# Lending result rooms to the Winograd weights, later residual copies, and ScalarE alone at the last eviction

## The chip, the cores and the metric

The kernel runs on one core of a Trainium2 chip. The metric is the time of one execution on the device in microseconds; several runs are made and their median is taken. One more execution is profiled, and everything called a view (busy shares, waits, the chain of waits, timelines, DMA queues) comes from that one. PE is TensorE, PEld its weight loads, DVE is VectorE, ACT is ScalarE, POOL is GpSimd, SP is SyncE, which only issues DMAs.

## The reference

Input is x, 16 images of 1024 channels by 32x32 pixels, all in float32. Two bottleneck layers follow each other:

```python
# layer 0
h = relu(bn(conv1x1(x, w_conv1)))            # 1024 -> 256
q, k = relu(bn(conv1x1(h, wq))), relu(bn(conv1x1(h, wk)))
v = bn(conv1x1(h, wv))
attn = softmax over the 9 neighbours of q . (k_neighbour + position), 32 heads of 8
h = relu(bn(sum over neighbours of attn * v_neighbour))
x = relu(bn(conv1x1(h, w_conv3)) + x)        # 256 -> 1024
# layer 1
y = relu(bn(conv1x1(x, w1)))                 # 1024 -> 256
y = relu(bn(conv3x3(y, w2)))                 # 256 -> 256
out = relu(bn(conv1x1(y, w3)) + x)           # 256 -> 1024
```

## The kernel before

The work is a written list of stages, run one after the other. A letter and an image name a stage: `C8` is the first convolution of image 8 (kind `conv1`, 8 parts, one for each 128 input channels, matmul line 389), `Q8` its q and k projections (kind `qk`, 5 parts, line 475), `V8` its v projection (kind `v`, 2 parts), `F3` layer 0's last convolution of image 3 fused with layer 1's first (kind `fused`, lines 421 and 389), `W0` the 3x3 convolution of images 0 to 3 in Winograd form (kind `wino`, 18 steps, line 822), `U0` layer 1's last convolution of image 0 (kind `u3`, 8 parts, line 421). `S12` to `S15` (kind `pairs`, lines 1263 and 1251) do that for the last four images with fewer products; their last piece is `Quad.finish`. The list begins `P0 P1 P2 P3 C4 F0 Q4 V4 F1 P5 P6 F2 P7 F3 C8 Q8 W0 V8 C9 U0 Q9 V9 U1 U2 U3`; P stands for C, Q and V of one image.

Attention and the Winograd transforms run on VectorE beside these stages. What is done after each part is written out by hand as a string of letters (`ORDER`), which `side.passes()` reads, one word after each part.

*Weights.* A queue holds the weight pieces in the order of use. `more_weights` takes the first, takes a room of 128x1024 and issues its load on SP (line 132). Rooms come from `wpool` with 5 buffers, or, for pieces named `U` (the transformed 3x3 weights, 18 pieces of 512 KB in a Winograd stage), from the list `spare` if it holds something. `done_with`, called after the last product that uses a piece, gives a lent room back to `spare` and calls `more_weights`. Before the changed version only `lend_rooms` fills `spare`, ahead of W12, with two other tiles cut in four.

*Results.* `rpool` has 4 buffers (`RESULTS`) for the outputs of the fused, `u3` and `pairs` stages. From C8 to the end of C9 no stage of that kind runs.

*Data.* `more_loads` issues loads on GpSimd (line 361) into the 5 rooms of `xpool` in the order of use, as rooms come free: `x` for C, `s` and `r` (residuals) for F and U, `V` (transformed images) for W. A transform on VectorE (lines 751 to 762) stores its `v` pieces through SP (line 787), and a V load waits for those stores.

*Residuals.* PSUM is used as 4 tiles of 128x1024 (`ps`), handed out in turn. Before the products of F or U, ScalarE copies the residual into a PSUM tile (`Expand.seed`, line 412) and the matmuls add to it. The first two such copies of a stage are issued in the last two parts of the stage before, each ahead of its part. Then `result` (line 440) evicts on ScalarE, with bias and ReLU, and GpSimd stores (line 441).

*Projection.* If an image is over 4 and its `Q` stage is followed by `V` and then C or U (`together`), its parts are: k, k, q, q, first v; then the `V` stage: part 0 the products of q with the position table (`positions`, line 521) and their copy (line 529), part 1 the second v. Each projection takes a PSUM tile and is evicted on ScalarE (line 488).

*Tail.* `Quad.finish` splits the last result in two halves in two PSUM tiles; before the change ScalarE evicts the first (line 1334) and VectorE the second (line 1337), and the second is stored by two DMAs of 64 partitions, on ACT and SP.

Of the kernel before, what the change touches and what calls it, by code (L numbers as in the profile page):

```python
# [8 lines left out]
F32 = mybir.dt.float32  # L9
AF = mybir.ActivationFunctionType  # L10
ALU = mybir.AluOpType
AX = mybir.AxisListType

P = 128
B, C, H, W = 16, 1024, 32, 32
HW = H * W
# [8 lines left out]
RELU = AF.Relu  # L25
CHUNKS, RESULTS = 5, 4
# [46 lines left out]
def sa_bottleneck_kernel(ctx: ExitStack, tc: tile.TileContext, x, w1t, wqkvt, w3t, u1t, u2t, u3t, params, out):  # L73
    nc = tc.nc
# [6 lines left out]
    rpool = ctx.enter_context(tc.tile_pool(name="rpool", bufs=RESULTS))  # L81
# [16 lines left out]
    queue, pieces, last_use = [], {}, {}  # L98

    def source(name, half):  # L100

        if name[0] == "U":
            return uw[int(name[1]), half]
        if name in ("w3", "u3"):
            return ws[name == "u3", half]
        if name[1] == "1":
            src = {"w1": w1t, "u1": u1t}[name].rearrange("(c p) n -> p c n", p=P)
            return src[:, half * NC // 2 : (half + 1) * NC // 2]
        at = {"wqk": slice(0, 2 * WID), "wv": slice(2 * WID, 3 * WID)}[name]
        return wqkvt.rearrange("(c p) n -> p c n", p=P)[:, :, at]  # L110

    def more_weights():

        if not queue:
            return
        key = name, of, half = queue.pop(0)
        if spare and name[0] == "U":
            t = lent[key] = spare.pop(0)
        else:
            t = wpool.tile([P, HW], F32, tag="w", name=f"{name}{half}_{of[0]}")  # L120
        src = source(name, half)
        n, k = src.shape[-1], 1
        for d in src.shape[1:-1]:
            k *= d
        view = t[:, : k * n].rearrange("p (c n) -> p c n", n=n)
        if len(src.shape) == 4:
            view = t.rearrange("p (m j o) -> p m j o", m=NW, j=2)
        if of[1] == 0 and name == "w1":
            for part in (slice(0, 1), slice(1, k)) if half == 0 else (slice(0, k),):
                nc.sync.dma_start(view[:, part], src[:, part])  # L130
        else:
            nc.sync.dma_start(view, src)
        pieces[key] = view
# [10 lines left out]
    spare, lent, late_room = [], {}, {}  # L144

    def lend_rooms():

        late_room["qc"] = apool.tile([P, HEAD_DIM, JPIX], F32, tag="qc", name="qc").rearrange("p d w -> p (d w)")
        for t in (late_room["qc"], kp.rearrange("p n r w -> p (n r w)")):
            spare.extend([t[:, :HW], t[:, HW : 2 * HW]])  # L150
        for _ in range(len(spare)):
            if queue and queue[0][0][0] == "U":
                more_weights()

    now = [0]

# [166 lines left out]
    def halves(half):  # L323
        return slice(half * HALF, (half + 1) * HALF)
# [613 lines left out]
    class Side:  # L938
# [71 lines left out]
        def finish(self, b):  # L1010
            self.passes()
            while any(job[0] == b for job in self.jobs):
                self.attention()
# [11 lines left out]
    for text in (  # L1025
# [5 lines left out]
        for word in text.split():  # L1031
            b, _, of = word[1:].partition(":")
            for letter in "CQV" if word[0] == "P" else word[0]:
                kind = {"C": "conv1", "Q": "qk", "V": "v", "F": "fused", "W": "wino", "U": "u3", "S": "pairs"}[letter]
# [6 lines left out]
    def together(b):  # L1041
        at = [(kind, c) for kind, c, of in stages].index(("qk", b))
        return b > FIRST and [kind for kind, c, of in stages[at + 1 : at + 3]] in (
            ["v", "conv1"], ["v", "u3"]
        )
# [185 lines left out]
    class Quad:  # L1231
# [65 lines left out]
        def finish(self, before, last_one):  # L1297
            self.product(1)
            self.add(0, 0, 1)
            before.product(2)  # L1300
            last_one.close()
            before.product(3)
            before.result(0, before.ends)
            self.product(6)
            self.add(1, 0, 6)
            self.room((7, 4))
            self.product(7)
            self.add(1, 1, 7)
            last_one.product(2)
            self.product(5)  # L1310
            self.split = []
            for n in range(2):
                self.add(n, 1, 5)
                t = psum.tile([P, HW], F32, tag="ps", name="ps")
                t = t.rearrange("p (b x) -> p b x", b=2)[:, :, : HALF // 2].rearrange("p b (j n) -> p b j n", j=2)
                self.split.append(t)
                seed = self.r[0].rearrange("p (b j n) -> p b j n", b=2, j=2)[:, :, :, n * HALF // 4 :][:, :, :, : HALF // 4]
                if n:
                    nc.vector.tensor_copy(t, seed)
                else:  # L1320
                    nc.scalar.activation(t, seed, AF.Identity)
            self.product(4)
            self.add(1, 0, 4)
            self.result(1, self.r[1])
            last_one.product(3)
            last_one.result(0, last_one.ends)
            t = rpool.tile([P, HW], F32, tag="r", name="result")
            for n in range(2):
                self.product(2, n)
                self.product(3, n)  # L1330
                to = t[:, halves(n)].rearrange("p (n b j) -> p n b j", b=2, j=2)
                of = self.split[n].rearrange("p b j n -> p n b j")
                if n == 0:
                    nc.scalar.activation(to, of, RELU, bias=self.shift[0], scale=1.0)
                    nc.sync.dma_start(self.to[0][:, halves(0)], t[:, halves(0)])
                else:
                    nc.vector.tensor_scalar(to, of, self.shift[0], 0.0, ALU.add, ALU.max)
            nc.scalar.dma_start(self.to[0][: P // 2, halves(1)], t[: P // 2, halves(1)])
            nc.sync.dma_start(self.to[0][P // 2 :, halves(1)], t[P // 2 :, halves(1)])

    def late_sums():

# [53 lines left out]
    hooks = {}  # L1396

    def run(at):
        now[0] = at
        kind, b, of = stages[at]  # L1400
        then = seeds(at + 1)
        for after in stages[at : at + 3]:
            if after[0] == "fused":
                next_fused[0] = after[1]
                break
        fetch_attended()
        if kind == "u3" and not late_room and any(s[0] == "wino" and s[1] == B - NK for s in stages[at + 1 : at + 3]):
            lend_rooms()
        if kind == "fused":
            parts, count = fused(b, of, then), 2 * NC  # L1410
        elif kind == "pairs":
            parts, count = late, len(of)
        elif kind == "u3":
            parts, count = last_sum(b, of, then), len(of)
        elif kind == "conv1":
            parts, count = first_conv(b), NC
        elif kind == "qk":
            parts, count = projections.setdefault(b, project(b)), 5
        elif kind == "v":
            parts, count = projections[b], 2  # L1420
        else:
            side.finish_firsts()
            if b == B - NK:
                late_weights()
            parts, count = winograd_conv(b), 18
        alone = kind not in ("fused", "u3", "pairs")
        for part in range(count):
            if alone and then and part >= count - 2 and kind != "wino":
                into, which = then[part - count + 2]

                if which not in into.ahead:
                    into.seed(which)
            next(parts)
            if part == 0 and kind == "fused" and stages[at + 1][0] == "fused":
                next_fused[0] = stages[at + 1][1]
            fetch_attended()
            side.passes()
            if (kind, b, part) in hooks:
                hooks[kind, b, part]()
        if kind == "wino":  # L1440
            made.extend((b + k, n) for k in range(NK) for n in range(NW))
            for into, which in then:
                into.seed(which)
# [11 lines left out]
    def at_first():  # L1455
        warm_up()
        more_weights()
        more_loads()
        nc.scalar.dma_start(par, params)
        more_weights()  # L1460
        norms()
        load_taps(0)
        more_weights()
        load_taps(1)
        more_weights()
        member_table()
        nc.gpsimd.memset(kp, 0.0)
        load_scaled()
        scale_rows()
        position_table()  # L1470
        side.first(winograd_weights())
        side.first(scale_weights())
        hooks["conv1", 2, 0] = clear_hidden

    at_first()
    for at in range(len(stages)):
        run(at)
# [40 lines left out]
```

## Time and profile before

| | us |
|---|---|
| median of 3 runs | 2364.34 |
| lowest, highest | 2363.7, 2369.66 |
| profiled execution, whole | 2365.22 |
| profiled execution, span of the core | 2363.5 |
| PE busy in the span | 2349.9 |
| DVE busy | 2155.0 |
| ACT busy | 916.1 |
| POOL busy | 491.2 |

The span runs from the first to the last instruction of the program; 1.7 us of the profiled execution lie outside it. The ends of matmuls are modelled, so two matmuls in a row overlap slightly in the timeline, and starts are better to compare than ends. A row of the waits gives who waited, for what, the total, how often and the longest. In a timeline the columns are start, duration, engine, line, operation, names, shapes and count, and in brackets the idle time before with what ended it. In the chain of waits they are start, duration and what the program's end depended on then. The trace's granted PE clock was 0.999 throughout.

### The profile page before, as it was taken

How to read it: one execution, taken by the hardware profiler on the slowest of the kernel's cores; microseconds unless marked ns; L12 is line 12 of the kernel's file. 1: busy time of each engine (PE TensorE's matmuls, PEld its weight loads, DVE VectorE, ACT ScalarE, POOL GpSimd, SP SyncE). 2: the span in 40 equal slices, each digit the busy share in tenths (PEclk: the TensorE clock that was granted, in tenths of full speed). 3: DMA queues.
4: the chain of work that ended last, by engine and by line, in shares of the span. 5: the costliest groups of instructions: out<-in, count | busy, mean ns of one | idle time of the engine just before them, and what ended most of it. 6: DMA issues, size and time to landing. Idle time of an engine off the chain costs nothing.

```text
span 2363.5 us, 18841 instructions
## 1 busy us (share of the span) xinstructions
PE 2349.9 (99%) x6252; PEld 1140.5 (48%) x6252; DVE 2155.0 (91%) x1771; ACT 916.1 (39%) x872; POOL 491.2 (21%) x901
## 2 busy tenths in 40 slices
PE   9999999999999999999999999999999999999998
PEld 4444444444475444444466444444467444444843
DVE  4899999999989999999989999999989999967686
ACT  3323342324122574443122574324222463444266
POOL 2212121212121331111121232111111231111222
PEclk9999999999999999999999999999999999999999
DMA  9968687878797998687887998688787897699887
GB/s 365 375 211 301 245 289 250 286 271 273 262 350 250 343 389 301 218 266 242 256 313 270 330 387 317 225 273 288 262 294 273 328 376 245 211 327 329 316 310 289
DMA packets 295584, 691.63 MB, mean 293 GB/s; under 512 B 20800, under 2 KB 165184, under 8 KB 286784
## 3 DMA queue, kind: packets, MB, share of 16 engines
q0 software_dynamic: 120032, 471.66, 54.7%
q1 hardware_dynamic: 174800, 217.54, 28.3%
q10 hardware_dynamic: 656, 1.23, 0.2%
q8 instruction: 50, 0.82, 0.1%
q14 instruction: 46, 0.38, 0.0%
HBM read 415.32 MB, written 275.03 MB: 292 GB/s over the span
## 4 chain that ended last, share of the span: by engine, by line
PE 95%; DMA 2%; DVE 2%; ACT 0%; issue 0%; DVEq 0%; SPq 0%; ACTq 0%
PE ps L389 36%; PE ps L421 33%; PE ps L475 13%; PE ps L822 9%; PE ps L1263 4%; DMA U<-uw 1%; DMA uw<-u 1%; DMA g<-in_u2t_dram 1%; PE ps L521 0%; DVE z L848 0%; DVE y L848 0%; ACT kp L488 0%; DVE prod L620 0%; DMA x<-in_x_dram 0%; DVE u L287 0%
## 5 line engine op out<-in xcount | busy, mean ns | idle before, releaser
L389 PE MATMUL ps<-result,u 128*128 128x512 f32 x1024 | 457.9, 592 | 0.0
L421 PE MATMUL ps<-a,w 128*128 128x512 f32 x1024 | 457.7, 592 | 0.0
L389 PE MATMUL ps<-x,w 128*128 128x512 f32 x1024 | 443.3, 593 | 0.7 <-DMA x<-in_x_dram 0.6
L677 DVE TENSOR_TENSOR acc<-e,bnv 128x2048 f32<-128x2048 f32 x144 | 327.5, 2283 | 18.4 <-ACT e L659 15.4
L421 PE MATMUL ps<-y,u 128*128 128x512 f32 x768 | 331.1, 592 | 0.0
L620 DVE TENSOR_TENSOR prod<-qc,bnk 128x2048 f32<-128x2048 f32 x144 | 324.0, 2287 | 1.8
L440 ACT ACTIVATE result<-ps,par 128x1024 f32<-128x1024 f32 x128 | 142.4, 1113 | 457.3 <-PE ps L421 394.4
L389 PEld LDWEIGHTS ps<-x,w 128*128 128x128 f32 x1024 | 194.6, 190 | 246.6 <-issue 243.6
L421 PEld LDWEIGHTS ps<-a,w 128*128 128x128 f32 x1024 | 194.6, 190 | 244.9 <-issue 243.5
L389 PEld LDWEIGHTS ps<-result,u 128*128 128x128 f32 x1024 | 194.3, 190 | 245.4 <-issue 238.0
L695 DVE TENSOR_TENSOR acc<-acc 128x2048 f32<-128x2048 f32 x128 | 293.4, 2292 | 4.4
L421 PEld LDWEIGHTS ps<-y,u 128*128 128x128 f32 x768 | 145.9, 190 | 183.3 <-issue 181.1
L475 PE MATMUL ps<-h,wqk 128*128 128x512 f32 x512 | 222.4, 592 | 0.5 <-ACT h L1095 0.5
L441 POOL DMA_DIRECT2D r<-result x128 | 68.7, 537 | 596.9 <-ACT result L440 592.9
L625 DVE TENSOR_TENSOR prod<-prod 128x2048 f32<-128x2048 f32 (+1 forms) x80 | 166.2, 2077 | 2.2
L475 PEld LDWEIGHTS ps<-h,wqk 128*128 128x128 f32 x512 | 97.1, 190 | 123.4 <-issue 111.2
L440 ACT ACTIVATE result<-ps,bn_sh 128x1024 f32<-128x1024 f32 x96 | 106.7, 1112 | 105.3 <-PE ps L421 103.9
L1095 ACT ACTIVATE h<-ps,par 128x1024 f32<-128x1024 f32 x32 | 38.4, 1202 | 260.8 <-PE ps L389 260.8
L412 ACT ACTIVATE ps<-s 128x1024 f32<-128x1024 f32 x128 | 131.3, 1025 | 15.1 <-DMA s<-in_x_dram 12.6
L488 ACT ACTIVATE kp<-ps,par 128x1024 f32<-128x1024 f32 x64 | 77.3, 1209 | 147.7 <-PE ps L475 118.5
L361 POOL DMA_DIRECT2D x<-in_x_dram x126 | 67.0, 533 | 275.5 <-PE ps L389 206.3
L845 ACT ACTIVATE z<-ps 128x1024 f32<-128x1024 f32 x48 | 49.1, 1024 | 179.3 <-PE ps L822 133.3
(373 smaller groups left out, 2655.3 us busy)
## 6 DMA issues: line engine op xcount, KB each, us to landing
s<-in_x_dram POOLq DMA_DIRECT2D x128, 512.0 KB, 5.9
r<-result POOLq DMA_DIRECT2D x128, 512.0 KB, 4.6
x<-in_x_dram POOLq DMA_DIRECT2D x126, 512.0 KB, 5.3
out_dram<-result POOLq DMA_DIRECT2D x126, 512.0 KB, 6.8
r<-r POOLq DMA_DIRECT2D x111, 512.0 KB, 7.0
v<-v SPq DMA_DIRECT2D x96, 408.0 KB, 4.8
U<-uw SPq DMA_DIRECT2D x60, 512.0 KB, 5.6
bnk<-kp SPq DMA_DIRECT2D x32, 680.0 KB, 6.9
```

The source lines that it names most:

```text
L389: nc.tensor.matmul(ps[n][:, halves(half)], wt[:, c % (NC // 2), n * P : (n + 1) * P], src[:, halves(half)], start=(c == first), stop=(c == ...
L412: nc.scalar.activation(ps, loaded.pop((self.kind, self.b, o)), AF.Identity)
L421: nc.tensor.matmul(self.ahead[o][:, halves(half)], pieces[key][:, n, o % (NC // 2) * P :][:, :P], self.src[:, n, halves(half)], start=Fals ...
L440: nc.scalar.activation(to_, ps, RELU, bias=self.shift(o), scale=1.0)
L475: nc.tensor.matmul(ps[:, halves(half)], pieces[key][:, m, at : at + P], h[:, m, halves(half)], start=(m == 0), stop=(m == NW - 1),)
L488: nc.scalar.activation(dst, src, func, bias=col(f"L0_conv_{name}_b", n), scale=col(f"L0_conv_{name}_s", n),)
L620: nc.vector.tensor_tensor(by_row(t[:, two]), by_row(qc), kc[:, :, i : i + JROWS, j : j + W], ALU.mult)
L625: nc.vector.tensor_add(u[:, :, 0:4], u[:, :, 0:4], u[:, :, 4:8])
L677: nc.vector.tensor_tensor(by_row(dst), rows(e[:, k, :]).unsqueeze(1).to_broadcast([P, HEAD_DIM, JROWS, W]), vc[:, :, i : i + JROWS, j : j ...
L695: nc.vector.tensor_add(acc, acc, t)
L822: nc.tensor.matmul(acc[i][:, at, :, n, :], pieces[key][:, m, at, n * P : (n + 1) * P], v[:, at, :, m * (TILES + TR) :][:, :, :TILES], star ...
L1263: nc.tensor.matmul(ps, w, by, start=i in (1, 7), stop=True, skip_group_check=True)
```

## The change

There are three edits.

1. After part 2 of stage C8 a hook, `lend_results`, runs four times over: it moves the first `U` piece of the queue to the front, takes a tile of `rpool`, puts it into `spare` and calls `more_weights`. During W0 `done_with` hands these four rooms on to further `U` pieces. At the end of every Winograd stage `spare` is emptied.
2. For a `V` stage that is `together` and followed by a `u3` stage (V9, V12, V15), the two first residual copies are issued later: the first after part 0 (the position products), the second after part 1.
3. In `Quad.finish` ScalarE evicts both halves; the first is stored by SP as before, the second by ACT in one DMA of 128 partitions.

```diff
+    def lend_results():
+
+        for _ in range(RESULTS):
+            at = [key[0][0] for key in queue].index("U")
+            queue.insert(0, queue.pop(at))
+            spare.append(rpool.tile([P, HW], F32, tag="r", name="lent"))
+            more_weights()
...
                 of = self.split[n].rearrange("p b j n -> p n b j")
-                if n == 0:
-                    nc.scalar.activation(to, of, RELU, bias=self.shift[0], scale=1.0)
-                    nc.sync.dma_start(self.to[0][:, halves(0)], t[:, halves(0)])
-                else:
-                    nc.vector.tensor_scalar(to, of, self.shift[0], 0.0, ALU.add, ALU.max)
-            nc.scalar.dma_start(self.to[0][: P // 2, halves(1)], t[: P // 2, halves(1)])
-            nc.sync.dma_start(self.to[0][P // 2 :, halves(1)], t[P // 2 :, halves(1)])
+                nc.scalar.activation(to, of, RELU, bias=self.shift[0], scale=1.0)
+                by = nc.scalar if n else nc.sync
+                by.dma_start(self.to[0][:, halves(n)], t[:, halves(n)])
...
-            if alone and then and part >= count - 2 and kind != "wino":
-                into, which = then[part - count + 2]
+            late_seeds = kind == "v" and together(b)
+            if alone and then and part >= count - (1 if late_seeds else 2) and kind != "wino":
+                into, which = then[0 if late_seeds else part - count + 2]
 
                 if which not in into.ahead:
                     into.seed(which)
             next(parts)
+            if late_seeds and then and part == count - 1:
+                into, which = then[1]
+                into.seed(which)
...
         if kind == "wino":
+            spare.clear()
             made.extend((b + k, n) for k in range(NK) for n in range(NW))
...
         hooks["conv1", 2, 0] = clear_hidden
+        for b, part in ((8, 2),):
+            hooks["conv1", b, part] = lend_results
```

## The prediction

> **What bounds the kernel now.** I read the page's busy shares first: TensorE is busy 99% of the span, so all that any edit can return is the idle time of PE, 2363.5 - 2349.9 = 13.6 us, start and tail included.
>
> ```profile
> PE 2349.9 (99%) x6252; PEld 1140.5 (48%) x6252; DVE 2155.0 (91%) x1771; ACT 916.1 (39%) x872; POOL 491.2 (21%) x901
> ```
>
> The waits of PE name where it stands still in mid-span; two of these rows are what the diff touches.
>
> ```profile
> PE ps L822 <- DMA U<-uw: 1.5, 1, 1.5
> PE ps L822 <- issue: 1.3, 1, 1.3
> ...
> PE ps L475 <- ACT kp L488: 1.0, 3, 0.3
> ...
> PE ps L822 <- ACT z L845: 0.2, 1, 0.2
> ```
>
> Third, the PE timeline of the first Winograd stage (W0, line 822). A step of 16 matmuls normally starts 3.45 us after the one before:
>
> ```profile
> 675.46 3.62 PE L822 MATMUL ps<-V__1_2446,U 128*128 128x256 f32 x16
> 680.61 3.69 PE L822 MATMUL ps<-V__2_2461,U 128*128 128x256 f32 x16 [1.54 <-DMA U<-uw]
> 684.14 3.62 PE L822 MATMUL ps<-V__2_2534,U 128*128 128x256 f32 x16
> ```
>
> 680.61 - 675.46 = 5.15, so 1.70 us is lost here, and 0.08 more in the step after. The chain of waits says why the fifth weight is late:
>
> ```profile
> 665.73 0.02 SPq L132
> 665.74 0.03 issue
> 665.77 14.70 DMA U<-uw
> ```
>
> Its load is issued only when the key weights' room comes free and takes 14.70 us in a full queue (DMA share over 1.0 from 658 to 690 in the windows). The stage lasts 664.99 to 729.55 = 64.56 us; W4, without a stall, 1207.29 to 1269.56 = 62.27. The excess is 2.29: the 1.78 above, and 0.52 around the step at 725.99, where ScalarE's copy waits for VectorE (line 848).
>
> Fourth, a projection followed by a `u3` stage (V9, V12, V15), on PE and then on ACT:
>
> ```profile
> 808.61 1.09 PE L521 MATMUL ps<-q,pos 64*32 64x512 f32 x16
> 810.03 3.70 PE L475 MATMUL ps<-h,wv 128*128 128x512 f32 x8 [0.33 <-ACT kp L488]
> 813.57 16.90 PE L421 MATMUL ps<-y,u 128*128 128x512 f32 x39
> ```
>
> ```profile
> 808.76 1.21 ACT L488 ACTIVATE kp<-ps,par 128x1024 f32<-128x1024 f32 x1 [2.28 <-PE ps L475]
> ```
>
> From the position products to the next stage: 813.57 - 808.61 = 4.96 us. P10, which has no residual copies there, takes 1164.98 - 1160.42 = 4.56. So each of three such places loses 0.40.
>
> Last, the tail:
>
> ```profile
> 2355.71 1.21 DVE L1291 TENSOR_SCALAR result<-bnk,bn_sh 128x1024 f32<-128x1024 f32 x1
> ...
> 2355.88 0.69 ACT L1334 ACTIVATE result<-ps,bn_sh 128x512 f32<-128x512 f32 x1
> ...
> 2356.85 0.73 DVE L1337 TENSOR_SCALAR result<-ps,bn_sh 128x512 f32<-128x512 f32 x1
> ...
> 2357.62 0.55 ACTq L1338 DMA_DIRECT2D out_dram<-result  x1
> 2357.86 1.18 SPq L1339 DMA_DIRECT2D out_dram<-result  x1
> ```
>
> PE ends at 2356.43, but VectorE is still on the 1024-wide eviction and starts the last half at 2356.85; SP issues the last store at 2357.86, which needs 4.6 us (DMA view): 2362.5.
>
> **What the Trainium skill says.** "DMA: Bandwidth & Descriptors", section "Anatomy of one DMA — SWDGE (gpsimd) path": a semaphore wait of a DMA is held on the issuing sequencer; the engines only drain queues. The trace agrees: SP stood 17.6 us on `a<-acc` (line 699) until 634.03, and the second `U` load behind it left at 634.46. Same page, "Issuing engines are not separate DMA queues": SP's and GpSimd's transfers interleave on the same 16 engines. The trace agrees: in the W0 crowd U loads took 14.7 and V loads up to 11.3 us, against medians of 7.6 and about 6 for the stretch.
>
> **The change part by part.**
>
> *Lent rooms.* After part 2 of image 8's first convolution four U loads of 512 KB come on SP, behind `a<-acc`, so at about 634.5 to 636.5; their four rooms (last stored at 617.47, that store landing some 3 us later) are free. The order of SP's queue in the changed kernel puts them there, then one U, then the six `v<-v` stores. So 5 of W0's weights land by about 645 and the fifth no longer waits for room: the step at 680.61 may start at 675.46 + 3.45 = 678.91. What is late next? (a) ScalarE's copies: that of the third step ends at 677.76 + 1.02 = 678.78, just in time; that of the fourth, held by VectorE, ends at 681.46 + 1.02 = 682.48, while its bank is wanted at 682.36: up to 0.2 lost. (b) V data of the sixth step: issued 670.72, 10.4 us to landing = 681.1, wanted at 682.4, 1.2 to spare. (c) Later steps have 2 us and more. Also, U loads in W0 now wait for the same step that frees a lent room, one fewer is in flight around 668.7, so (b) should rather come earlier. VectorE's last chain starts at 699.26 after 2.70 idle, released through ScalarE by PE; it moves with PE, so the 0.52 stays. Gain 1.78 - 0.2, taken as **1.5** (bounds 0 and 2.1). Added DMA bytes: none; 2.1 MB move to 634-650.
>
> What they are moved past: six `v<-v` stores (643.18 to 653.28) and the two `bnk` stores. Unused DMA share from 638 to 650 is 0.25, 0.52 and 0.57 of 4 us each = 5.4 us; four loads at the 403 GB/s or so of a full queue need 2.1/0.403 = 5.2 us. They just fit. VectorE waits once (1.08 us at 646.20) for such a store; I allow 1 us of delay. Image 8's x loads, the last issued at 633.44 and wanted at 646.7, have 5 us over.
>
> *Residual copies.* Three places. With the position products' bank taken before the first copy, the last v product gets the bank of the second q product, evicted by 1345.29 + 1.20 or its like, over 3 us earlier, and not that of v's first part. Removes 0.33 of wait and the slower restart: 3 x 0.40 = **1.2** (bounds 0.9 and 1.3). The second copy now follows v's last eviction: v's last product ends near 813.2, eviction 1.21 to 814.5, copy 1.02 to 815.5, wanted by the second product at 813.2 + 3.43 = 816.6; 1.1 to spare. Behind it on ScalarE stand a third copy (816.5, wanted at 820.0) and the first result (its products end at 816.6). On GpSimd one residual load passes behind five position stores (2.85 us): later by about 3 us, wanted over 10 us later. Nothing on PE.
>
> *Tail.* VectorE loses its 0.73; ScalarE evicts the second half right after the first, at about 2356.50, done 0.69 later at 2357.2 and not 2357.58. One store of 256 KB goes from ScalarE at 2357.2; SP loses its third. With the 4.2 to 4.6 us that stores of 128 and 256 KB took there, landing is 2361.4 to 2361.8 against 2362.5. The bytes are the same and the engines were full until 2361, so I take **0.7** (0.3 to 1.1).
>
> Sum: 1.5 + 1.2 + 0.7 = 3.4 us. The profiled execution had 2365.22 (span 2363.5 and 1.7 around it), so 2361.8 on its scale; it stood 0.9 over the median of the runs, 2364.34, on whose scale I predict 2360.9. Does a gain at 680 survive to the end? VectorE idles 13.5 us at 2075-2089 and 4.2 at 2152, and attention outputs arrive 20 us and more before their stages, so later stages move with PE.
>
> **The rivals.**
>
> *The stall moves on.* In W12, which already borrows rooms for its weights, PE stood 1.3 us ("issue" above) in the same sixth step, for a V load. If in W0 that V load, or the copy held by VectorE, ends last by as much, the lent rooms give nothing: 1.9 us from the rest, 2362.4. For it: the spare time is 1.2 us only. Against: W0's GpSimd queue has no output stores, W12's had several.
>
> *The loads crowd out the stores.* If the whole 5.2 us lands ahead of the `v<-v` stores, the transform on VectorE waits, the sixth V load lands at 686.3 for 682.4, and 3.9 is lost where 1.78 was: +2.1 in W0, +0.2 in all, slower from 5.0 us of delay on, and up to 2366.4 should the tail and the copies also return nothing. For it: only 0.2 us of unused share is left over. Against: most of the burst drains before 643.18.
>
> *The tail doesn't move*, because 1.5 MB of stores are in flight from 2356 on whoever evicts: 2361.6; part of the forecast's range.
>
> **How the numbers follow.** Forecast 0.62 (2359.5 to 2362.0), moved stall 0.20, crowd-out or some wait of its kind 0.18. The range 2358.8 to 2366.0 takes in the bounds and the crowd-out. About 0.3% (7.1 us) is what a measurement of this kernel can tell from no change. PE's idle time in the touched places is under 6 us, so faster by that much has 0.03; slower by that much needs crowding beyond the price above, which I give 0.09; within, 0.88.
>
> **What would show it.** Right: no `DMA U<-uw` row among PE's waits, W0 at 62.8 us or so, 4.56 us at each of the three projections, the last store landing under 6 us after PE's end. Wrong: a wait of line 822 for V or z over 1 us, V loads of W0 issued later than 663.41, a new wait of line 421 for a residual copy.

## The result, and the profile after

The changed kernel takes **2371.52 us** (median of 7 runs, 2370.04 to 2376.23) against 2364.34 before: 7.2 us slower, ratio 1.0035 with a 95% interval of 1.0025 to 1.0045. The forecast was 2360.9, 3.4 us faster. The profiled execution has a span of 2368.5 us, 5.0 more than before.

Busy shares, from the page after:

```profile
PE 2351.1 (99%) x6252; PEld 1142.1 (48%) x6252; DVE 2155.1 (91%) x1770; ACT 916.7 (39%) x873; POOL 491.2 (21%) x901
```

No engine has more work to speak of; PE is idle 17.4 us and not 13.6. The waits of PE after (who waited, for what, total, times, longest) name the place:

```profile
PE ps L830 <- ACT z L853: 6.3, 2, 6.0
PE ps L483 <- ACT h L1103: 1.6, 1, 1.6
PE ps L1462 <- DVE warm L1459: 1.3, 1, 1.3
PE ps L830 <- issue: 1.1, 1, 1.1
```

The edits move the lines by 8: L822 is L830 now, L845 (the z copy) L853, L475 L483. The U wait and the three waits of L475 for `kp` have gone, as forecast. But a wait of 6.0 us for a z copy (ScalarE copies a product out of PSUM, and PE may write there again) stands in W0, where 0.2 stood. The timeline of PE in W0, after:

```profile
675.93 3.62 PE L830 MATMUL ps<-V__1_2454,lent 128*128 128x256 f32 x16
685.57 5.46 PE L830 MATMUL ps<-V__2_2469,lent 128*128 128x256 f32 x16 [6.02 <-ACT z L853]
690.87 3.62 PE L830 MATMUL ps<-V__2_2542,U 128*128 128x256 f32 x16
```

The weights of the fifth step are `lent` and on time. Its V load is on time too: it landed at 677.03. Its place in PSUM is not. The step starts 9.64 us after the one before (5.15 in the kernel before), and then takes 5.30 to the next start, not 3.45. W0 lasts 665.47 to 736.29 = **70.82 us** against 64.56. The chain of waits, after, leads back from there:

```profile
667.15 0.53 POOL V__2_2469 L369
667.68 1.52 POOL q L556 x2
669.20 0.70 POOL pos L541
669.90 1.60 POOL pos L547 x3
671.50 12.77 DMA pos<-by_offset
...
684.49 1.03 ACT z L853
```

`V_1_2` is the V load of the fifth step (here V__2_2469, in the kernel before V__2_2461), `V_2` that of the sixth. Read upward: the z copy waits for a position store of image 8 to land, since that store still reads the room (`zpool`, three rooms) that z takes; the store stands on GpSimd's queue behind the q stores and `V_1_2`, which left at 667.15. In the kernel before, by GpSimd's timeline:

```profile
663.41 0.53 POOL L361 DMA_DIRECT2D V__2_2461<-v  x1 [9.17 <-DMA v<-v]
```

Ahead of `V_1_2` the chain after names a U load that left at 657.48. That is not what released it, since the U load landed at 667.68, when `V_1_2` had left. The sixth v store, which `V_1_2` waits for, left at 657.03 and landed at 666.51 (653.28 and 662.86 before). So two of the prediction's signs of being wrong are there, a z wait over 1 us and a V load later than 663.41. Why that store was late is on VectorE, in its timelines before and after:

```profile
646.20 1.01 DVE L762 TENSOR_TENSOR v<-form 128x816 f32<-128x816 f32 x1 [1.08 <-DMA v<-v]
```

```profile
649.95 1.01 DVE L770 TENSOR_TENSOR v<-form 128x816 f32<-128x816 f32 x1 [4.93 <-DMA v<-v]
```

The transform waits 4.93 us and not 1.08 for its first store to land (the v pieces lie in `zpool` too). That store left SP at 643.08 (643.18 before) and landed at 649.85 (646.1 before). Last, the windows before and after, four microseconds each (length; busy time of PE, PEld, DVE, ACT and POOL; PE clock, DMA share, GB/s):

```profile
634.00:638.00 4.00, 4.00 (x10) 1.74 (x10) 3.90 (x7) 0.00 (x0) 0.00 (x0) 1.00 0.91 256
638.00:642.00 4.00, 4.00 (x11) 1.72 (x10) 3.93 (x5) 0.00 (x0) 0.00 (x0) 1.00 0.75 309
642.00:646.00 4.00, 4.00 (x11) 1.85 (x10) 3.04 (x4) 0.00 (x0) 0.00 (x0) 1.00 0.48 141
646.00:650.00 4.00, 4.00 (x11) 1.68 (x10) 3.74 (x4) 1.21 (x1) 0.00 (x0) 1.00 0.43 128
```

```profile
634.00:638.00 4.00, 4.00 (x11) 1.79 (x10) 3.90 (x6) 0.00 (x0) 0.45 (x1) 1.00 1.00 323
638.00:642.00 4.00, 4.00 (x10) 1.71 (x9) 3.93 (x5) 0.00 (x0) 0.00 (x0) 1.00 1.01 373
642.00:646.00 4.00, 4.00 (x11) 1.80 (x10) 2.94 (x4) 0.00 (x0) 0.00 (x0) 1.00 1.01 406
646.00:650.00 4.00, 4.00 (x11) 1.81 (x10) 0.05 (x1) 0.89 (x1) 0.00 (x0) 1.00 0.92 241
```

The DMA engines are full until 646, where before they had a share of 0.91, 0.75 and 0.48. In the last row VectorE is busy 0.05 of 4 us (3.74 before): that is the transform standing still.

From the starts of all 6252 matmuls in both traces, the 5.0 us of span are: start of the program +0.5, W0 +6.3, the three projections -1.3, later stages -0.3, tail -0.2.

### The profile page after: what moved, and what is told of

It reads as the page before. It is cut to its first block, busy times and chain, and to the rows that moved or that the text cites. A ratio compares the mean times of both kernels' runs of the same rounds, so it can differ in the third digit from the quotient of the medians.

```text
span 2368.5 us, 18844 instructions
## 1 busy us (share of the span) xinstructions
PE 2351.1 (99%) x6252; PEld 1142.1 (48%) x6252; DVE 2155.1 (91%) x1770; ACT 916.7 (39%) x873; POOL 491.2 (21%) x901
## 4 chain that ended last, share of the span: by engine, by line
PE 92%; issue 3%; DMA 2%; DVE 1%; POOL 1%; ACT 0%; POOLq 0%; SPq 0%; ACTq 0%; DVEq 0%
PE ps L397 36%; PE ps L429 32%; PE ps L483 14%; PE ps L830 9%; DMA g<-in_u2t_dram 1%; PE ps L529 1%; POOL out_dram L1303 1%; DMA pos<-by_offset 1%; DMA U<-uw 0%; DVE z L856 0%; DMA pc<-r 0%; DVE y L856 0%; POOL r L369 0%; DVE prod L628 0%; DVE z L860 0%
## 5 line engine op out<-in xcount | busy, mean ns | idle before, releaser
L483 PE MATMUL ps<-h,wqk 128*128 128x512 f32 x512 | 222.4, 592 | 1.6 <-ACT h L1103 1.6
L483 PEld LDWEIGHTS ps<-h,wqk 128*128 128x128 f32 x512 | 97.1, 190 | 124.4 <-issue 111.2
L853 ACT ACTIVATE z<-ps 128x1024 f32<-128x1024 f32 x48 | 49.1, 1024 | 185.5 <-PE ps L830 133.2
```

Source lines behind the costliest of these rows:

```text
L483: nc.tensor.matmul(ps[:, halves(half)], pieces[key][:, m, at : at + P], h[:, m, halves(half)], start=(m == 0), stop=(m == NW - 1),)
```

## The experiments

**Theory A**: the four loads of 512 KB, ahead of the v stores on SP, delay them; this runs on through `V_1_2`, the position stores and z to PE. **Rival B**: the residual copies or the last eviction cost the time. **Rival C**: the lending itself does (other rooms, other releases). **Rival D**: PE really waits for the V data. The times of the kernel before, measured beside each group of runs, were 2364.29, 2363.97 and 2364.23.

### no_lend: without the first edit

```diff
-        for b, part in ((8, 2),):
-            hooks["conv1", b, part] = lend_results
```

> The changed kernel without its first edit (no rooms lent); the later residual copies and the new last eviction stay. Theory A (the four loads delay the v stores, and with them everything behind): W0 as before, 64.5 us, with the wait of 1.5 us for U back and the first wait of DVE L770 for a v store back at about 1.1 us; the three projections 4.55 us each; in all 1.2 from the copies and 0.2 from the tail, so about 1.4 us under the kernel before, and 8 to 9 us under the changed one. Rival B (the later residual copies or the last eviction cost time that the profiles hide): at or above the kernel before by 2 us or more.

Measured: 2362.45 (13 runs), ratio 0.9992 (0.9984 to 1.0000). L770 waits 1.09. W0 takes 64.03. B falls: the other two edits cost no time, and the whole loss, 2371.52 - 2362.45 = 9.1 us, belongs to the first. The U wait in W0 is back, but smaller than expected, 1.02 us. The view names a V load as its end, V__2_2534; that is the load of the sixth step, and it landed at 680.17, when PE had started (679.94). The U load landed at 679.80. PE waits there on the semaphores of the U load and of `V_1_2`, and the number of the second is used again by V__2_2534, hence the wrong name.

### idle_loads: the traffic without the lending

The kernel before, with this run after part 2 of C8:

```diff
+        for i, half in ((2, 0), (1, 1), (2, 1), (1, 2)):
+            t = rpool.tile([P, HW], F32, tag="r", name="idle")
+            nc.sync.dma_start(t.rearrange("p (m j o) -> p m j o", m=NW, j=2), uw[i, half])
```

> The kernel before plus four loads of 512 KB into the same four rooms at the same place of SP's queue (after part 2 of C8, behind a<-acc); nothing ever reads them, and W0 has no lent rooms. This is the traffic without the lending. Theory A: the v stores land some 3 us later as in the changed kernel, the load V_1_2 leaves at about 667 and not 663.4, the copy z waits for the position stores, PE stands some 6 us in the fifth step of W0, W0 takes 70 to 71 us and the whole is 5.5 to 7 us above the kernel before (no U wait beside it, since it is hidden behind the z wait). Rival C (the lending itself: other rooms, other releases, SP waiting for PE in W0): W0 64.6 us, the whole within 0.7 us of the kernel before.

Measured: 2374.28 us (5 runs), ratio 1.0039 (1.0026 to 1.0051). Timelines of VectorE and PE of this kernel (L768 is before's form of L770, L828 that of W0's matmuls):

```profile
649.19 1.01 DVE L768 TENSOR_TENSOR v<-form 128x816 f32<-128x816 f32 x1 [4.32 <-DMA v<-v]
```

```profile
686.61 5.45 PE L828 MATMUL ps<-V__2_2469,U 128*128 128x256 f32 x16 [7.20 <-ACT z L851]
```

`V_1_2` left at 666.37, W0 took 72.0 us, one more than expected. The span is 7.5 over before's and the median 10.0 (5.5 to 7 expected), so the size is not met, and by more in the medians than in the one profile. But loads that nobody reads make the same stall at the same place, so the lending is not needed for it; C falls.

### lend_act: the four loads ten microseconds earlier, from ScalarE

```diff
-    def more_weights():
+    def more_weights(by=None):
...
-            nc.sync.dma_start(view, src)
+            (by or nc.sync).dma_start(view, src)
...
-            more_weights()
+            more_weights(nc.scalar)
```

(the last change only in `lend_results`)

> The changed kernel with one difference: the four first loads into the lent rooms are issued by ScalarE, which is idle from 624.2 to 648.6, and so leave some 10 us earlier, into unused DMA time, not behind a<-acc on SP. The lending in W0 is as in the changed kernel. Theory A: they land by about 634, the first wait of DVE L770 for a v store is 1.1 us or less, the V_1_2 load leaves at about 663.4 plus 0.5, no z wait over 1 us, no wait for U, W0 62.6 to 63.2 us; the whole 2361.0 to 2361.9, that is 2.5 to 3.4 us under the kernel before. A risk inside A: the last x loads of C8 or C9 or the acc stores meet the burst instead, and PE waits for x. Rival C (the lending itself): W0 stays near 70 us.

Measured: 2362.11 (21 runs), ratio 0.9990 (0.9983 to 0.9996). The loads left at 623.30 to 624.72 and had landed by 631.36. VectorE, this kernel:

```profile
646.10 1.01 DVE L770 TENSOR_TENSOR v<-form 128x816 f32<-128x816 f32 x1 [1.08 <-DMA v<-v]
```

`V_1_2` left at 663.24, no U wait, W0 62.78 us: the same lending loses nothing when its first loads come at another time and from another queue, as A has it. The median was 0.2 above the expected range.

### pos_act: position stores from ScalarE

```diff
+        by = nc.scalar if b == 8 else nc.gpsimd
...
-                nc.gpsimd.dma_start(room[n], q[:, n, :].rearrange("p (j w) -> p j w", j=NJ))
+                by.dma_start(room[n], q[:, n, :].rearrange("p (j w) -> p j w", j=NJ))
```

and `by` for both position stores alike.

> The changed kernel, with the two q stores and five position stores of image 8 issued by ScalarE and not by GpSimd, so that they no longer stand behind the late V_1_2 load. Theory A, with the position stores as the link: they leave at 666.7 to 669.4 and not 669.2 to 672, land by about 680, the z copy of the third step starts by about 681 and not 684.5. Then the next late thing decides: the load V_2 of the sixth step, which is issued only when V_1_2 has landed (677.0) and lands at about 686.4, for a step that is due at 683; so PE waits there some 3 us in place of 6.0, and W0 falls from 70.8 to 66.5 to 69 us. Rival D (V_1_2 itself is what PE waited for): PE's start of that step does not move, W0 stays at 70.8.

Measured: 2373.56 (4 runs), ratio 1.0037 (1.0024 to 1.0051): a miss, and a poor experiment. Timelines of ScalarE and PE in it:

```profile
669.47 7.25 ACTq L548 DMA_DIRECT2D pos<-by_offset  x4
676.85 1.94 ACT L854 ACTIVATE z<-ps 128x1024 f32<-128x1024 f32 x2 [10.64 <-DMA pos<-by_offset]
```

```profile
677.92 6.47 PE L831 MATMUL ps<-V__1_2448,lent 128*128 128x256 f32 x16 [5.75 <-ACT z L854]
```

ScalarE's own queue was held in the stores: the chain puts their issue at 675.93 down to the landing of a U load issued at 658.91 on SP. The z copies stood behind them on the same engine, so PE's stall moved to the third step. D is not settled by this run.

### pos_src: position stores that do not read z's room

```diff
-            by_offset = by_offset.rearrange("p (j w) -> p j w", j=NJ)
+            of = q[:, 0, :] if b == 8 else by_offset
+            by_offset = of.rearrange("p (j w) -> p j w", j=NJ)
```

> The changed kernel, in which the five position stores of image 8 read q's tile and not the copy by_offset (so image 8's attention gets wrong position terms: that part of the computation is left wrong). The number, size, queue and order of all stores stay; only the z copy of the third step no longer waits for them, since they do not read the room that it takes. Theory A, position stores as the last link: the z wait of 6.0 us in the fifth step goes. V_1_2 lands at about 677 for a step then due at 679.5, so that step is in time; next is the load for the sixth step, which leaves only when V_1_2 has landed and lands at about 686.4 for 683: PE waits there 3 to 4 us, restarts slowly, and W0 takes 66 to 68.5 us; the whole 2 to 4.5 us under the changed kernel. Rival D (PE waits for the V data in the fifth step, and the z wait is only its shadow): PE still stands in the fifth step and W0 stays at 70 to 71.

Measured: 2369.12 (20 runs), ratio 1.0021 (1.0015 to 1.0028), 2.4 us under the changed kernel. PE in W0, this kernel:

```profile
690.07 5.12 PE L831 MATMUL ps<-V__2_2542,U 128*128 128x256 f32 x16 [4.77 <-issue]
```

The z wait is gone from the fifth step, though `V_1_2` left and landed no earlier (10.0 us in flight, 9.9 in the changed kernel): D falls, as it does by the landing of `V_1_2` in the changed kernel, 8.5 us before the step that it is for. The position stores were the link. PE then stands in the sixth step. The profile names no releaser ("issue"), but `V_2` landed at 689.98, 0.09 us before. So a second wait stood right behind the first, 1.3 us shorter. W0 took 69.22, 0.7 more than expected.

### lend_1, lend_2, lend_3: the dose

```diff
-        for _ in range(RESULTS):
+        for _ in range(1):
```

and 2 and 3 likewise.

> The changed kernel with one room lent in place of four: one added load of 512 KB behind a<-acc on SP, three fewer. Theory A: the loads are landed by about 643, so the first v store (issued at 643.1) still lands by 646.5; first wait of DVE L770 1.0 to 1.5 us, V_1_2 leaves at 663.5 to 664.2, no z wait over 1 us. One weight more is there ahead of W0, so the U wait is gone or under 0.5: W0 62.8 to 63.8, the whole 2361.0 to 2362.8. Rival C (the lending itself): W0 at 66 us or more, whatever the number of rooms.

> The changed kernel with two rooms lent. Theory A, by 1.25 us of landing for each load: the last of the loads lands at about 645 (648.2 with four), so the first v store lands at 646.5 to 647.5 and DVE L770 waits 1.3 to 2.5 us; V_1_2 leaves at 663.8 to 665, behind it the position stores by 0.3 to 1.3 us, and the z copy by somewhat more: PE waits 0 to 2.5 us for z, W0 63 to 66 us, between lend_1 and the changed kernel and not in proportion: nearer to lend_1.

> The changed kernel with three rooms lent. With no room, one, two and four, the first wait of DVE L770 for a v store was 1.09, 1.08, 1.73 and 4.93 us. Theory A: each load more costs about 1.25 us of the engines' time ahead of that store once their unused time is spent, so with three it waits about 3.0 to 3.7 us, V_1_2 leaves at 664.5 to 666, the z copy of the third step is 1 to 4 us later than with two, and PE waits 1 to 4 us for it: W0 64 to 68 us, so between the 62.8 with two and the 70.8 with four; the whole 2363 to 2368. Rival E (a step, not a slope: the fourth load alone does it, for instance through the room that it takes): W0 62.8 with three as with two.

| rooms | time, us (runs) | ratio, 95% | wait of L770 | W0 |
|---|---|---|---|---|
| 0 (no_lend) | 2362.45 (13) | 0.9992 (0.9984 to 1.0000) | 1.09 | 64.03 |
| 1 | 2362.61 (12) | 0.9993 (0.9984 to 1.0001) | 1.08 | 62.79 |
| 2 | 2361.87 (12) | 0.9992 (0.9984 to 1.0000) | 1.73 | 62.77 |
| 3 | 2367.88 (12) | 1.0010 (0.9998 to 1.0022) | 3.68 | 68.86 |
| 4 (changed) | 2371.52 (7) | 1.0035 (1.0025 to 1.0045) | 4.93 | 70.82 |

VectorE with three rooms:

```profile
653.02 1.01 DVE L770 TENSOR_TENSOR v<-form 128x816 f32<-128x816 f32 x1 [3.68 <-DMA v<-v]
```

PE waits 4.41 us for the z copy in the fifth step there. W0 was 0.2 us under its expected range with two rooms and 0.9 above it with three. The store's delay is a slope that starts after the first load; a step at the fourth room (rival E) is out. W0's loss has a threshold between two and three: 0.65 us of delay is absorbed, 2.6 is not (in the profile of lend_2b below, with a wait of 1.83, PE waits 0.11 for the same copy).

### lend_after_v: the same loads behind the v stores

```diff
-        for b, part in ((8, 2),):
-            hooks["conv1", b, part] = lend_results
+        hooks["conv1", 8, 7] = lend_results
```

> The changed kernel with its hook at the last part of C8, so that the four loads stand on SP behind the six v stores and not ahead of them (they leave at about 654). Theory F (it is the order: small stores behind large loads): the v stores are not delayed, L770 waits 1.1 us, V_1_2 leaves by 663.6 and W0 takes under 65 us. Theory A as it was found (any 2 MB more ahead of the V loads, q and position stores in a full queue delay them): from 652 on the DMA share is over 0.95 already, the loads take 5 us of it ahead of V_1_2 and the position stores, so L770 is on time but the position stores land 3 to 5 us later than the 677.5 of the kernel before; PE waits 2 to 5 us for z, and W0 takes 66 to 70 us.

Measured: 2362.25 (20 runs), ratio 0.9991 (0.9984 to 0.9998). Theory F holds, and the wider form of A falls. GpSimd's and SP's timelines of this kernel, whose W0 starts at 669.53, 4.5 us later than before's because its program started so much later:

```profile
667.49 0.53 POOL L369 DMA_DIRECT2D V__2_2461<-v  x1 [9.34 <-DMA v<-v]
```

```profile
658.44 3.88 SPq L132 DMA_DIRECT2D lent<-uw  x4
662.42 0.65 SPq L508 DMA_DIRECT2D bnk<-kp  x1
```

With 2.1 MB more in a stretch that was nearly full already, `V_1_2`, issued later than they but on GpSimd, landed in 7.0 us (6.8 before), and the last position store at 682.45, which is 677.9 on before's scale (677.53). What paid is SP's own queue: the `bnk` store of 662.42 landed 20.2 us later, at 682.66 (13.3 in the kernel before), and no engine waited for it. W0 took 63.44. So the bytes hurt where they stand ahead on the same queue, and what is hurt matters only if an engine waits for it. No run sends the four loads at 634 from another queue than the v stores', so it is not shown that the queue alone, at the same time, would have saved them.

### best: another queue for the last image's first half

lend_act, and in the tail:

```diff
-                by = nc.scalar if n else nc.sync
+                by = nc.scalar if n else nc.gpsimd
```

> lend_act (the four loads issued by ScalarE at 623) with one more difference: the store of the last image's first half is issued by GpSimd, which is free then, and not by SP, where it stands behind the store of line 1300 (issued 1.55 us after PE's last start). It then leaves some 0.8 us after that start. If the last landing is held up by the order of issue on SP, the time from PE's last matmul start to the last landing falls from 6.3 to 5.7 to 6.1 us and the whole to about 2361.7; if the 16 engines' rate for the last 1.5 MB sets it, 6.2 to 6.4 and no difference from lend_act (2362.1).

Measured: 2362.83 (13 runs), ratio 0.9999 (0.9991 to 1.0007). GpSimd was still issuing its store of line 1303 and sent the half 1.29 us after the start of PE's last two matmuls. From that start to the last landing it is 6.36 us, lend_act has 6.29: nothing gained. But the half left only 0.27 us sooner than it did on SP (1.56 in lend_act), so the test is a weak one.

### lend_2b and no_lend_b: is the lending worth anything

Copies of lend_2 and no_lend, on one chip.

> lend_2 once more (two rooms lent), beside no_lend_b on the same chip, to size what the lending itself is worth where it crowds nothing out. By the profiles W0 takes 62.77 us with two rooms and 64.03 without: 1.0 to 1.7 us less than no_lend_b, at about 2361.5 to 2362.5. If it is 0.5 us or less, a later stage takes that gain back.

> no_lend once more (the residual copies and the last eviction alone), for the comparison with lend_2b: 1.2 to 1.9 us under the kernel before, and 1.0 to 1.7 above lend_2b.

Measured: 2362.18 and 2362.17 (22 runs each), ratios 0.9986 (0.9978 to 0.9993) and 0.9989 (0.9981 to 0.9997). No difference, against the 1.0 to 1.7 expected. PE at the fifth step without lending, in this second profile:

```profile
678.88 3.69 PE L830 MATMUL ps<-V__2_2461,U 128*128 128x256 f32 x16 [0.16 <-DMA V__2_2534<-v]
```

The name in brackets is wrong here too: that V load landed at 679.02, the U load at 678.75. The stall was 1.54 in the profile of before, 1.02 in no_lend's, 0.16 here, so in this execution there was little to gain. W0 took 63.19, and 63.42 with two rooms. Whether a later stage takes some of the gain back is open: in these two profiles the sixth step of W12 starts 5.01 us after the fifth with two rooms and 4.02 without. Over all profiles this time varies from 3.87 to 6.19 with rooms lent in W0, and from 4.02 to 4.88 without.

## Why the prediction was wrong

*The step that failed* is "They just fit", in the part on what the lent loads are moved past. I set 5.2 us of loads against 5.4 us of unused share **up to 650**, though the first v store leaves at 643.18 and VectorE wants it at 645. Free time after that moment is no room for what stands ahead of it. From the windows of before, shown above, what was unused before 643.18 is 0.09 x 4 + 0.25 x 4 + 0.52 x 1.18 = 2.0 us, so 5.2 - 2.0 = 3.2 us of the burst were still ahead of the store. With one load nothing is left over, with two 0.6, with three 1.9. Measured above the 1.09 of no_lend: 0, 0.6, 2.6 and 3.8. This estimate was made after the runs, and why three and four loads cost 0.6 to 0.7 more than it says is open. The "1 us of delay" that I allowed was 3.8, and "most of the burst drains before 643.18" was wrong: the four loads landed from 642.02 to 647.08, the U load behind them at 648.31, and the store at 649.85.

*The rival "the loads crowd out the stores"* had the mechanism. Its number, the sixth V load at 686.3, came out (686.42) by luck: I had the whole 5.2 us at the v store, whereas `V_1_2` left 3.7 late, then took 3.1 longer, and `V_2` behind it 1.6 less. And I let PE be late only there. The position stores behind `V_1_2` on GpSimd, which my steps for W0 did not list, were later still: z at 684.49 held the fifth step. The line of before that claim (a) was read from names them:

```profile
677.76 1.02 ACT L845 ACTIVATE z<-ps 128x1024 f32<-128x1024 f32 x1 [4.53 <-DMA pos<-by_offset]
```

The copy already waited for a position store there and ended only 0.1 us before PE was to start, so a late position store had next to no time to spare. And I had the loss as 3.9 with no slow restart, and decided against it at 0.18 with the argument above. The loss was 6.0 of waiting and 5.30 - 3.45 = 1.85 of restart. From 5.0 us of delay on it would be slower, I wrote; 3.8 at the store was enough: the last position store left 2.7 us later than before (671.50 against 668.80) and landed 6.7 later. Why it then took 12.8 us and not 8.7 is open.

*Claim (a)*, that the z copy of the third step comes "just in time", and *claim (b)*, V data of the sixth step at 681.1, both presumed an undisturbed queue. In lend_act, where it is, they hold: the copy starts at 677.42, `V_2` lands at 680.01, and W0 is at 62.78 where 62.8 was the sign of being right.

*The gain of 1.5 for the lent rooms* was oversized even where nothing is crowded out. It priced one stall from one profiled execution (1.70 us). That stall varies from 0.16 to 1.54 between the profiles of before, no_lend and no_lend_b, and in the medians the lending is worth 0.0 (lend_2b against no_lend_b).

*Residual copies*: right. The three places take 819.90 - 815.35 = 4.55 us and the same at the others (4.56 forecast), 1.3 in all. PE after, at the first:

```profile
815.35 1.09 PE L529 MATMUL ps<-q,pos 64*32 64x512 f32 x16
816.37 3.70 PE L483 MATMUL ps<-h,wv 128*128 128x512 f32 x8
819.90 0.59 PE L429 MATMUL ps<-y,u 128*128 128x512 f32 x1
```

*Tail*: 0.2 to 0.3 and not 0.7. From the start of PE's last two matmuls to the last landing it was 6.65 us, is 6.38. The issues of the last stores, after (ACT has the second half, SP at line 1343 the first):

```profile
2362.24 0.34 SPq L1300 DMA_DIRECT2D out_dram<-result  x1
2362.37 0.35 ACTq L1343 DMA_DIRECT2D out_dram<-result  x1
2362.67 0.38 SPq L1343 DMA_DIRECT2D out_dram<-result  x1
```

The second half is evicted sooner, but it is no longer the last to land: the first half's store, behind that of line 1300 on SP, lands at 2367.40, the second at 2366.77. My own doubt ("the engines were full until 2361") was the better guide.

In sum, a gain of 3.4 was forecast as 1.5 + 1.2 + 0.7; in the profiled execution the three came out as -6.3, +1.3 and +0.2. By the medians the kernel without the first edit is 1.8 to 2.1 us under the one before. lend_act, lend_2b, no_lend_b and lend_after_v (ratios 0.9986 to 0.9991, all intervals below 1) beat both kernels, by 2.0 to 2.2 us against the one before, where the profiles show 1.5 for the copies and the tail, and can't be told from each other. No run has the copies or the tail alone.

## What to carry to other kernels

When transfers are put ahead of others on a queue, count the unused DMA time only up to the moment when the first transfer behind them is issued, and name the engine that waits for that transfer; a burst that would fit over the whole stretch can still be late by most of its length. Then follow everything that stands behind the late instruction on each queue in turn, stores as well as loads: a store that must land before its source is written again is a wait like any other. Check a releaser that a view names against its landing time: one that landed after the wait ended did not end it. And before a stall is taken as a gain, see whether it has the same length in a second execution.

## What the runs showed of the hardware

*Two queues share the engines; within a queue what stands ahead counts.* The Trainium skill, "DMA: Bandwidth & Descriptors", section "Queues, rings and completion order", says that a DMA engine takes turns between queues packet by packet. lend_after_v fits that: loads on SP's queue left GpSimd's V load at 7.0 us (6.8 before) while SP's own next store took 20.2 (13.3 before). The changed kernel put the loads and the stores that VectorE needs on one queue.

*Restart at half speed.* After 6.02 us of idling the sixteen matmuls took 5.30 us. The windows of the changed kernel show the clock (the figure after the five busy times):

```profile
679.60:685.50 5.90, 0.00 (x0) 0.00 (x0) 0.00 (x0) 1.01 (x1) 1.61 (x3) 0.73 1.03 416
685.50:689.00 3.50, 3.43 (x8) 2.80 (x9) 3.42 (x5) 0.82 (x2) 0.00 (x0) 0.50 1.02 413
```

The Trainium skill, "TensorE: Matmul & The Clock Gate", section "What's actually happening", gives half the clock after an idle stretch of about 3.4 us, and the full clock again after a busy one as long. 0.50 over 3.5 us agrees. But 0.73 over the idle stretch means that the clock fell after about 2.7 us of it, sooner than the page has it (3.9 to 4.5 us in idle_loads, lend_3, pos_src and pos_act, by the clock records of their traces). The 1.02 us stall in no_lend cost no such restart: its step took 3.52 us to the next start. With idle times of 4.4 to 7.2 us the runs here paid 1.5 to 1.9 us, and pos_act 2.9. That is about half of the time that PE then ran at 0.50, by the same records: 2.9 to 3.6 us, and 5.6 in pos_act.

*At most eight transfers, in this program.* In the changed kernel the load `V_2` left GpSimd only when `V_1_2` had landed, by GpSimd's timeline:

```profile
677.59 0.58 POOL L369 DMA_DIRECT2D V__2_2542<-v  x1 [5.54 <-DMA V__2_2469<-v]
```

Between the two stand exactly seven others (two q, five position stores). In pos_act, where those seven are elsewhere, it left 0.54 us behind `V_1_2`, at 669.01. There three of ScalarE's stores were held instead: they left at 669.47, 675.30 and 675.93, each 0.02 us after the landing of the transfer that stood eighth before it in the order of SP and ScalarE together. The trace shows why: GpSimd's issues name eight landing semaphores in turn, SP's and ScalarE's together another eight, and an issue waits for the earlier transfer with its own number. In this program, then, an issue also waits for the landing of the eighth transfer before it; that comes from the program's semaphores, and no run here tells of a limit of the chip. So a late landing holds later issues that have nothing to do with it.

*The start of the program varies* by about 5 us between executions of nearly the same kernel (a wait of 2 us for ScalarE near 35 us, and a restart after it), and the stall of W12's sixth step from 0.25 to 2.6. So I read differences under 1 us from the stage and not from the total.
